# PSUM banks dealt in turn in an attention stage: maxima and short work share four banks, values' products in halves, the first maxima four heads at once

## The chip, the cores and the metric

The kernel runs on one core of a Trainium2 chip as a single launch. The metric is the device time of that launch in microseconds, the median over several runs; lower is better. One execution was also recorded by the hardware profiler. In the text PE is TensorE, PEld its weight loads, DVE VectorE, ACT ScalarE, POOL GpSimd and SP SyncE.

## The reference

A network of eight sublayers works on x (4 batches of 512 tokens, 512 features). Each sublayer is added as x + tanh(g) · sublayer(layernorm(x)). The seventh, called stage 6 in the kernel, is the one that changes. It is attention of each batch's 512 tokens to 512 context tokens, with 32 heads of 16 features and a rotary position on queries and keys:

```python
q = (x @ Wq).reshape(b, n, 32, 16)
k, v = jnp.split(ctx @ Wkv, 2, axis=-1)        # each (b, 512, 32, 16)
q = apply_axial_rope(q, pos_map)
k = apply_axial_rope(k, ctx_pos_map)
logits = jnp.einsum('bqhd,bkhd->bhqk', q, k) * 0.25
w = jax.nn.softmax(logits, axis=-1)
attn = jnp.einsum('bhqk,bkhd->bqhd', w, v).reshape(b, n, 512)
return attn @ Wout + bout

x = x + jnp.tanh(g_xattn[3]) * _L3_xattn_ref(_layernorm(x), ctx, pos, pos, Wq, Wkv, Wout, bout)
```

## The kernel before

Stages 0 to 5 come first, stage 7 (a mixture of experts) after it. Everything is float32. Keys and values of stage 6 are worked out in earlier stages and lie in DRAM as k6 and v6. The results of stage 5 lie in DRAM too: its last block is scattered there by an indirect DMA from GpSimd's queue (s_ys from s_yb), and stage 6 loads them per 128 tokens (s_y from s_ys, a buffer of two tiles) and adds them to x (L729).

**Start.** `pieces(b)` yields the short work that makes a batch's queries: `results` (load and add stage 5's results, then `lnstats`, whose inverse square root is a Newton iteration on DVE), `xT` (normalise on DVE at L1576, transpose into ptx), `query` (product pq, then rope on DVE, L1427 to L1429) and `queryT` (transpose into ptq, copied on ACT into qT). For batch 0 all pieces run ahead of the loop; for batch b+1 they are handed out between the slots of batch b.

**Softmax.** Logits are needed twice. `maxima` computes them with the queries on the partitions (s_ps, 128x512 per head and 128 queries), and DVE takes each row's maximum, negated, into `top` (L1656). When a group of four heads is through, `turn` transposes these maxima (ptm) and adds them to the queries' transpose qT (L1631) in a spare feature. The second time the logits come with the keys on the partitions and the maximum already taken off (s_pl), and ACT takes their exps into pr (L1766). `weigh` multiplies the exps by the values (s_av, an accumulation over the four key tiles, with a column of ones for the sums), ACT copies av to oT, and `norm` transposes it (pt), takes the reciprocal of the sums (L1703) and multiplies (L1704). `project` (ptr) and `projected` (po) apply the output matrix; bias and residual follow on DVE (L1724, L729).

**Loop.** Per batch there are eight groups g of four heads, in each four key tiles k, in each two slots (i = 1, then 0): 64 slots. A slot issues together two logits products for two heads and two maxima products of a group twelve slots ahead (LEAD = 12). Each of the four has a contraction of 32 rows and sits in its own quarter of PE's rows. The program order on PE is fixed for everything that goes through `together` (products and values' products); transpositions and projections are placed by the scheduler. Ahead of the loop the twelve first pairs of maxima run alone.

`later` holds the values' product of a key tile, flushed in the next slot with i = 1. `behind` holds norm, project and projected, flushed two at a time in slots with i = 0.

**Banks.** Of PSUM's eight banks of 128x512 float32 the maxima have three (tag sc, with ptx, ptq and the queries of batch 0), the logits three (pl), all other short work one (mm: ptm, pt, ptr, po, pq of later batches), av one. Two waits are written out by hand: a slot's first product waits for the first exp and the first maximum of the slot before:

```python
self.together(parts + more, list(freed) + exps[-2:-1])   # freed is freed[-2:-1]
```

Transposed maxima, normalised averages and the rest have a bank of their own, so a bank in which DVE still reads one of them holds up no maximum.

Of the kernel before, what the change touches and what calls it, by code (L numbers as in the profile page):

```python
# [9 lines left out]
F32 = mybir.dt.float32  # L10
# [38 lines left out]
class Net:  # L49
# [116 lines left out]
    def lnstats(self, name, tiles, key="", root=True):  # L166


        nc = self.nc
        n = len(tiles)  # L170
        mv = self.s(f"mv_{name}", 2 * n, f"mv{n}{key}")
        mv = mv.rearrange("p (t k) -> p t k", k=2)
        for i, x in enumerate(tiles):
            st = self.s(f"st_{name}_{i}", 6, "st")
            nc.vector.bn_stats(st, x)
            nc.vector.bn_aggr(mv[:, i, :], st)
        rs = self.s(f"rs_{name}", n, f"rs{n}{key}")
        if root:
            nc.scalar.activation(rs, mv[:, :, 1], AF.Sqrt, bias=self.eps[1e-5])
            nc.vector.reciprocal(rs, rs)  # L180
            return mv, rs
        v, y = self.s(f"nv_{name}", n, "nv"), self.s(f"ny_{name}", n, "ny")
        nc.vector.tensor_scalar(v, mv[:, :, 1], 1e-5, None, op0=ALU.add)
        ints = rs.bitcast(I32)
        nc.vector.tensor_scalar(ints, v.bitcast(I32), 1, None, op0=ALU.logical_shift_right)
        nc.vector.tensor_scalar(ints, ints, -1, 0x5F3759DF, op0=ALU.mult, op1=ALU.add)
        for _ in range(4):
            nc.vector.tensor_tensor(y, rs, rs, op=ALU.mult)
            nc.vector.tensor_tensor(y, y, v, op=ALU.mult)
# [33 lines left out]

    def transposed(self, name, src, dst, i=0, tied=False):

        pt = self.mm(f"ptr_{name}")
        for c in range(4):
            ins = self.nc.tensor.transpose(
                pt[:, c * P : (c + 1) * P], src[:, c * P : (c + 1) * P], self.ident
            ).ins  # L230
            if tied:
                self.tie(ins)
        self.evict(i, dst, pt.rearrange("p (c n) -> p c n", c=4))
# [1300 lines left out]
    def s6(self):  # L1534
# [13 lines left out]

        bank = lambda name: self.ps3.tile([P, S], F32, tag="sc", name=f"s6_{name}")

# [7 lines left out]
        def pieces(b):  # L1558
# [3 lines left out]
            made[b] = kT, qT, va  # L1562
            for y in range(2):
                nc.sync.dma_start(kT[y], self.k6[b][:, 4 * y : 4 * y + 4, :])
            nc.sync.dma_start(va, self.v6[b].rearrange("(k p) n -> p k n", p=P))
            xs = self.x[b * TB : (b + 1) * TB]
# [20 lines left out]
            def query(t):  # L1587
                if b:
                    pq = self.mm(f"s6_pq_{b}_{t}")
                else:  # L1590

                    pq = bank(f"pq_{b}_{t}")
                self.chain(pq, [(room["xT"][:, c, cols(t)], wq[:, c, :]) for c in range(DC)])
                self.rope(f"q_{b}_{t}", pq, b * TB + t, ropes[t % 2])

            def results():

                self.combine("s5", self.wt5, range(b * TB, (b + 1) * TB))
                stats[b] = self.lnstats(
                    f"s6_{b}", self.x[b * TB : (b + 1) * TB], f"s6{b}", root=False  # L1600
                )
# [16 lines left out]
        def maxima():  # L1618

            freed = []  # L1620

            def turn(b, g):
                qT = made[b][1][g // 4]
                pt = self.mm(f"s6_ptm_{b}_{g}")
                for t in range(TB):
                    nc.tensor.transpose(
                        pt[:, t * P : (t + 1) * P],
                        top[g % 2][:, t].rearrange("p j k -> p (j k)"),
                        self.ident,
                    )  # L1630
                nc.vector.tensor_tensor(qT[:, g % 4, :], qT[:, g % 4, :], pt, op=ALU.add)  # L1631

            waiting = None
            for b in range(NB):
                kT, qT = made[b][0:2]
                for g in range(8):
                    for t in range(TB):
                        for y in range(2):
                            if waiting and t == 1:
                                turn(*waiting)  # L1640
                                waiting = None
                            ps = [bank(f"ps_{b}_{g}_{t}_{y}_{i}") for i in range(2)]
                            parts = []
                            for i in range(2):
                                rows = slice(32 * (2 * y + i), 32 * (2 * y + i + 1))
                                parts.append((
                                    ps[i],
                                    qT[g // 4][rows, g % 4, t * P : (t + 1) * P],
                                    kT[g // 4][rows, g % 4, :],
                                    dict(start=True, stop=True),  # L1650
                                ))

                            def after(ps=ps, dst=top[g % 2][:, t, 2 * y : 2 * y + 2, 16:17]):
                                for i in range(2):
                                    with self.tc.high_priority():
                                        ins = nc.vector.tensor_reduce(  # L1656
                                            dst[:, i], ps[i], axis=AX.X, op=ALU.max, negate=True
                                        ).ins
                                    freed.append(ins)

                            yield parts, freed[-2:-1], after
                    waiting = b, g
            turn(*waiting)

        behind, later = Behind(), Behind()
        avs, o4s, exps = {}, {}, []

        def flush(what, n=None):
            last, what.waiting = what.waiting[:n], what.waiting[n:] if n else []
            for f, args in last:  # L1670
                f(*args)

        def weigh(b, g, k, prs):

            va = made[b][2]
            if k == 0:
                avs[g] = self.ps1.tile([P, S], F32, tag="av", name=f"s6_av_{b}_{g}", bufs=1)
            parts = []
            for j in range(4):
                h = 4 * g + j  # L1680
                parts.append((
                    avs[g][32 * j : 32 * (j + 1), :],
                    va[:, k, 17 * h : 17 * h + 32],
                    prs[j // 2][:, j % 2, :],
                    dict(start=(k == 0), stop=(k == TB - 1)),
                ))
            self.together(parts)
            if k == TB - 1:
                oT = self.t(f"s6_oT_{b}_{g}")
# [3 lines left out]
        def norm(b, g, oT):  # L1693
            if g == 0:
                o4s[b] = self.up.tile([P, TB, D], F32, tag="o", name=f"s6_o_{b}")
            po = self.mm(f"s6_pt_{b}_{g}")
            for t in range(TB):
# [15 lines left out]
        def project(b, t):  # L1713
            oT = self.t(f"s6_oTT_{b}_{t}").rearrange("p (c n) -> p c n", c=DC)
            self.transposed(f"s6_o_{b}_{t}", o4s[b][:, t, :], oT, 1)
            behind(projected, b, t, oT, more=True)
# [3 lines left out]
        def projected(b, t, oT):  # L1720
            po = self.mm(f"s6_po_{b}_{t}")
            self.chain(po, [(oT[:, c, :], wo[:, c, :]) for c in range(DC)])
# [4 lines left out]
        for piece in pieces(0):  # L1727
            piece()
        nc.sync.dma_start(wo, a["s6_wo"].rearrange("(c p) n -> p c n", p=P))
        beside = maxima()  # L1730
        for _ in range(LEAD):
            parts, freed, after = next(beside)
            self.together(parts, freed)
            after()
        for b in range(NB):
# [4 lines left out]
            for g in range(8):  # L1740
                y, gi = g // 4, g % 4
                for k in range(TB):
                    prs = [None, None]
                    for i in (1, 0):


                        pl = [
                            self.ps3.tile([P, S], F32, tag="pl", name=f"s6_pl_{b}_{g}_{k}_{i}_{j}")
                            for j in range(2)
                        ]  # L1750
                        parts = []
                        for j in (2 * i, 2 * i + 1):
                            rows = slice(32 * j, 32 * (j + 1))
                            parts.append((
                                pl[j % 2],
                                kT[y][rows, gi, k * P : (k + 1) * P],
# [3 lines left out]
                        more, freed, after = next(beside, None) or ([], [], None)  # L1760
                        self.together(parts + more, list(freed) + exps[-2:-1])
                        prs[i] = self.up.tile(
                            [P, 2, S], F32, tag="pr", name=f"pr_s6_{b}_{g}_{k}_{i}", bufs=4
                        )
                        for j in range(2):
                            exps.append(nc.scalar.activation(prs[i][:, j, :], pl[j], AF.Exp).ins)  # L1766
# [85 lines left out]
def kernel(ctx: ExitStack, tc: tile.TileContext, a: dict, out: bass.AP):  # L1852
# [122 lines left out]
```

## Time and profile before

| | us |
|---|---|
| median of 3 runs | 3399.83 (3399.31 to 3401.43) |
| profiled execution | 3401.39 |
| its span in the profile | 3399.4 |
| stage 6: from the last scatter of stage 5 to the last projection | 2254 to 3014 |
| batches 0 to 3 of the loop begin at | 2342.1, 2501.1, 2670.9, 2840.7 |
| mean granted TensorE clock | 0.92 |

Busy in the whole span: PE 2880.1 (85%), PEld 1432.3 (42%), DVE 1975.8 (58%), ACT 1197.1 (35%), POOL 627.9 (18%). The profiled execution is 1.6 us above the median of the runs; sums are made against its own time. In a group of instructions the line gives busy time, mean ns of one, and the idle time of the engine just before with the instruction that ended it. In a timeline a line is: start, duration, engine, line of the kernel, output from inputs, shape, count, and in brackets the idle time before and what ended it.

### The profile page before, as it was taken

What the parts mean: (1) busy time and instruction counts of PE and PEld (TensorE: products, weight loads), DVE (VectorE), ACT (ScalarE), POOL (GpSimd) and SP (SyncE); (2) the same over time, 40 slices, a digit from 0 to 9 for tenths busy, and PEclk for the clock granted to TensorE, in tenths of its full rate; (3) what the DMA queues carried; (4) which work ended last, traced back from release to release, by engine and by line L of the source; (5) the groups of instructions that cost most, each with busy time, mean ns of one, the idle gap of its engine ahead of it and who ended that gap; (6) DMA issues with size and microseconds to landing.
All of it is one profiled execution on the core that took longest, in us unless ns stands there. A gap on an engine that the chain in (4) does not pass through costs nothing.

```text
span 3399.4 us, 39917 instructions
## 1 busy us (share of the span) xinstructions
PE 2880.1 (85%) x14620; PEld 1432.3 (42%) x14624; DVE 1975.8 (58%) x3148; ACT 1197.1 (35%) x1927; POOL 627.9 (18%) x509
## 2 busy tenths in 40 slices
PE   4889898968998989998836699968898988889995
PEld 2333333223444444444414588842233332244673
DVE  5555555558797989975687311137666666634103
ACT  1243333355544454433222111112544444520231
POOL 0000000005564655760000122210000000000341
PEclk9799999988998999999967699987999999989997
DMA  3000000047675876861212599971000000022698
GB/s 125 7 1 7 1 1 9 1 160 227 195 230 177 241 223 202 250 188 57 84 63 85 177 324 325 325 250 50 13 27 13 27 1 1 1 75 78 245 385 314
DMA packets 266338, 438.56 MB, mean 129 GB/s; under 512 B 32368, under 2 KB 114544, under 8 KB 264608
## 3 DMA queue, kind: packets, MB, share of 16 engines
q1 hardware_dynamic: 247776, 382.52, 35.3%
q0 software_dynamic: 13760, 45.10, 3.7%
q10 hardware_dynamic: 4608, 8.39, 0.7%
q8 instruction: 117, 1.92, 0.2%
q14 instruction: 77, 0.63, 0.1%
HBM read 370.79 MB, written 65.13 MB: 128 GB/s over the span
## 4 chain that ended last, share of the span: by engine, by line
PE 38%; DVE 9%; issue 3%; DMA 2%; POOL 2%; ACT 1%; SPq 0%; POOLq 0%; DVEq 0%; ACTq 0%
PE s_po L238 8%; PE s_pl L262 7%; PE pg_s L238 6%; PE s_av L262 4%; DVE s_top L1656 2%; PE s_ph L238 2%; PE s_pq L238 2%; PE s_ps L262 1%; PE s_pkv L238 1%; PE s_pr L238 1%; DVE x L729 1%; DMA s_y<-s_ys 1%; PE pt_s L218 1%; POOL s_ys L1321 1%; PE s_pb L238 1%
## 5 line engine op out<-in xcount | busy, mean ns | idle before, releaser
L1012 POOL TENSOR_TENSOR s_h<-s_h,s_C 128x512 f32<-128x512 f32 x256 | 447.2, 1747 | 295.7 <-DVE s_h L1011 249.7
L1656 DVE TENSOR_REDUCE s_top<-s_ps 128x1 f32<-128x512 f32 x512 | 330.1, 686 | 162.6 <-PE s_ps L262 158.4
L1766 ACT ACTIVATE pr_s<-s_pl 128x512 f32<-128x512 f32 x512 | 277.9, 595 | 344.2 <-PE s_ps L262 327.1
L1011 DVE TENSOR_TENSOR_SCAN s_h<-s_da,s_db 128x512 f32<-128x512 f32 x256 | 312.0, 1219 | 62.8 <-PE s_y L262 37.1
L262 PE MATMUL s_pl<-s_qT,s_kT 32*128 32x512 f32 x1024 | 291.4, 642 | 63.4 <-DVE s_top L1656 59.0
L262 PE MATMUL s_ps<-s_kT,s_qT 32*128 32x512 f32 x1024 | 306.6, 668 | 6.1 <-DVE s_top L1656 5.8
L1010 ACT ACTIVATE s_da<-s_rdl,s_A 128x512 f32<-128x512 f32 x256 | 184.3, 722 | 329.3 <-DVE s_h L1011 328.7
L238 PE MATMUL s_ph<-xT_s,s_wu 128*128 128x256 f32 x1024 | 250.4, 400 | 0.7 <-ACT xT_s L161 0.7
L771 PE MATMUL s_acc<-s_wd,s_hT 128*128 128x512 f32 x512 | 239.9, 612 | 6.8 <-ACT s_hT L802 6.8
L238 PEld LDWEIGHTS s_ph<-xT_s,s_wu 128*128 128x128 f32 x1024 | 199.9, 200 | 79.3 <-issue 48.4
L238 PEld LDWEIGHTS pg_s<-s_xbT,s_w 128*128 128x128 f32 (+1 forms) x1872 | 214.1, 183 | 19.8 <-issue 17.8
L599 DVE TENSOR_REDUCE s_nmx<-ps_s 128x2 f32<-128x992 f32 x128 | 151.4, 1184 | 116.7 <-PE ps_s L262 116.7
L238 PE MATMUL pg_s<-s_xbT,s_w 128*128 128x128 f32 (+1 forms) x1872 | 215.7, 275 | 1.4 <-ACT s_xbT L161 1.4
L262 PE MATMUL s_av<-pr_s,s_v 128*32 128x512 f32 (+1 forms) x1536 | 209.6, 617 | 0.8 <-ACT pr_s L1766 0.7
L1009 DVE TENSOR_TENSOR s_db<-s_B,s_rdu 128x512 f32<-128x512 f32 x256 | 202.7, 792 | 10.5 <-DMA s_B<-s_bc 2.7
L714 ACT ACTIVATE pr_s<-pl_s 128x1024 f32<-128x1024 f32 (+1 forms) x128 | 130.9, 1022 | 192.1 <-PE pl_s L262 161.7
L262 PE MATMUL s_y<-s_h,ident 64*64 64x512 f32 x1024 | 146.5, 635 | 47.1 <-issue 30.0
L1400 DVE TENSOR_TENSOR g_s<-g_s,pg_s 128x256 f32<-128x256 f32 x78 | 27.5, 353 | 263.9 <-ACT g_s L1399 263.9
L262 PEld LDWEIGHTS s_pl<-s_qT,s_kT 32*128 32x128 f32 x1024 | 80.0, 184 | 232.9 <-ACT pr_s L1766 197.7
L262 PE MATMUL pl_s<-s_qT,s_kT 32*128 32x512 f32 (+1 forms) x512 | 151.1, 667 | 26.1 <-ACT pr_s L714 23.0
L262 PE MATMUL ps_s<-s_kT,s_qT 32*128 32x496 f32 x512 | 156.1, 713 | 4.5 <-DVE s_nmx L599 4.1
L771 PEld LDWEIGHTS s_acc<-s_wd,s_hT 128*128 128x128 f32 x512 | 93.4, 192 | 151.9 <-issue 116.4
(376 smaller groups left out, 4269.7 us busy)
## 6 DMA issues: line engine op xcount, KB each, us to landing
s_B<-s_bc SPq DMA_DIRECT2D x256, 256.0 KB
s_C<-s_bc SPq DMA_DIRECT2D x256, 256.0 KB
s_w<-in_s_wg SPq DMA_DIRECT2D x39, 704.0 KB
s_w<-in_s_wu SPq DMA_DIRECT2D x39, 704.0 KB
s_w_rt<-in_s_ru SPq DMA_DIRECT2D x47, 512.0 KB
s_w_rt<-in_s_rd SPq DMA_DIRECT2D x47, 512.0 KB
s_w<-in_s_wd SPq DMA_DIRECT2D x39, 512.0 KB
s_y<-s_ys SPq DMA_DIRECT2D x32, 512.0 KB
```

The lines of the kernel that those rows point to most:

```text
L218: nc.tensor.transpose(pt[:, i * P : (i + 1) * P], xl[i][:, c * P : (c + 1) * P], self.ident)
L238: ins = self.nc.tensor.matmul(out, lhsT=l, rhs=r, start=(i == 0), stop=(i == len(pairs) - 1)).ins
L262: ins = self.nc.tensor.matmul(out, lhsT=l, rhs=r, **flags).ins
L599: i = nc.vector.tensor_reduce(nmx[:, at : at + 2], ps[:, :, 0:M], axis=AX.X, op=ALU.max, negate=True,)
L714: nc.scalar.activation(prs[i][0:n], pl[0:n], AF.Exp)
L771: ins = nc.tensor.matmul(accs[i][t], lhsT=hT[:, j, t * P : (t + 1) * P], rhs=wd[f // 4][:, f % 4, :], start=(f == 0), stop=(f == FC - 1),).ins
L1009: nc.vector.tensor_tensor(db, br, du, op=ALU.mult)
L1010: nc.scalar.activation(da, dl, AF.Exp, scale=am[:, e, n : n + 1])
L1011: nc.vector.tensor_tensor_scan(h, da, db, 0.0, op0=ALU.mult, op1=ALU.add)
L1012: nc.gpsimd.tensor_tensor(h, h, cr, op=ALU.mult)
L1656: ins = nc.vector.tensor_reduce(dst[:, i], ps[i], axis=AX.X, op=ALU.max, negate=True).ins
L1766: exps.append(nc.scalar.activation(prs[i][:, j, :], pl[j], AF.Exp).ins)
```

## The change

Seven edits, all in stage 6 except the first, which is in a helper that stage 6 uses:

- the Newton iteration of `lnstats` has three steps instead of four;
- the loads of keys and values of a batch are issued behind the loads of stage 5's results, not ahead of them;
- the tag sc has four banks and is dealt in turn to the maxima and to all short work (ptx, pq, ptq, ptm, pt, ptr, po); the tag mm is gone from the stage;
- the waits written out by hand name the reader of the very bank that a product takes (`dealt` and `read` keep the books), where that reader is a maximum or an exp;
- the twelve first pairs of maxima run as six double pairs, four heads at once, with the second pair of heads in the banks of the logits;
- the values' product of a key tile is issued as two halves of 256 tokens, one in each of the two slots that follow;
- in every slot one entry of `later` and one of `behind` is flushed.

```diff
-        for _ in range(4):
+        for _ in range(3):
...
-    def transposed(self, name, src, dst, i=0, tied=False):
+    def transposed(self, name, src, dst, i=0, tied=False, room=None):
-        pt = self.mm(f"ptr_{name}")
+        pt = (room or self.mm)(f"ptr_{name}")
...
-        bank = lambda name: self.ps3.tile([P, S], F32, tag="sc", name=f"s6_{name}")
+        banks = {"sc": 4, "pl": 3}
+        readers = {tag: [] for tag in banks}
+        def dealt(name, tag="sc"):
+            at = len(readers[tag])
+            readers[tag].append(None)
+            old = readers[tag][at - banks[tag]] if at >= banks[tag] else None
+            t = self.ps3.tile([P, S], F32, tag=tag, name=f"s6_{name}", bufs=banks[tag])
+            return t, (tag, at), [old] if old is not None else []
+        def read(where, ins):
+            readers[where[0]][where[1]] = ins
+        bank = lambda name: dealt(name)[0]
...
-            for y in range(2):
-                nc.sync.dma_start(kT[y], self.k6[b][:, 4 * y : 4 * y + 4, :])
-            nc.sync.dma_start(va, self.v6[b].rearrange("(k p) n -> p k n", p=P))
...
-                if b:
-                    pq = self.mm(f"s6_pq_{b}_{t}")
-                else:
-                    pq = bank(f"pq_{b}_{t}")
+                pq = bank(f"pq_{b}_{t}")
...
             def results():
                 self.combine("s5", self.wt5, range(b * TB, (b + 1) * TB))
+                for y in range(2):
+                    nc.sync.dma_start(kT[y], self.k6[b][:, 4 * y : 4 * y + 4, :])
+                nc.sync.dma_start(va, self.v6[b].rearrange("(k p) n -> p k n", p=P))
...
-                pt = self.mm(f"s6_ptm_{b}_{g}")
+                pt = bank(f"ptm_{b}_{g}")
...
-                            ps = [bank(f"ps_{b}_{g}_{t}_{y}_{i}") for i in range(2)]
+                            ps = [
+                                dealt(f"ps_{b}_{g}_{t}_{y}_{i}", "pl" if alone[0] and y else "sc")
+                                for i in range(2)
+                            ]
...
-                                    freed.append(ins)
-                            yield parts, freed[-2:-1], after
+                                    read(ps[i][1], ins)
+                            yield parts, olds, after
...
-        def weigh(b, g, k, prs):
+        def weigh(b, g, k, prs, half):
+            cols = slice(half * (S // 2), (half + 1) * (S // 2))
...
-            po = self.mm(f"s6_pt_{b}_{g}")
+            po = bank(f"pt_{b}_{g}")
...
-            self.transposed(f"s6_o_{b}_{t}", o4s[b][:, t, :], oT, 1)
+            self.transposed(f"s6_o_{b}_{t}", o4s[b][:, t, :], oT, 1, room=bank)
...
-            po = self.mm(f"s6_po_{b}_{t}")
+            po = bank(f"po_{b}_{t}")
...
-        for _ in range(LEAD):
-            parts, freed, after = next(beside)
-            self.together(parts, freed)
-            after()
+        for _ in range(LEAD // 2):
+            two = [next(beside) for _ in range(2)][::-1]
+            self.together(
+                [p for parts, _, _ in two for p in parts], [i for _, old, _ in two for i in old]
+            )
+            for _, _, after in two:
+                after()
...
-                        self.together(parts + more, list(freed) + exps[-2:-1])
+                        self.together(parts + more, freed + pl[0][2] + pl[1][2])
...
-                        if i == 1:
-                            flush(later)
-                            later(weigh, b, g, k, prs, more=True)
-                        else:
-                            idle = not behind.waiting
-                            flush(behind, 2)
-                            if idle and todo:
-                                todo.pop(0)()
+                        flush(later)
+                        if i == 0:
+                            for half in range(2):
+                                later(weigh, b, g, k, prs, half, more=True)
+                        idle = not behind.waiting
+                        flush(behind)
+                        if idle and i == 0 and todo:
+                            todo.pop(0)()
...
-    with net.pools(wp=2, kq=4, vp=2, up=1, rp=1, tp=8, bp=1, sp=2, ps3=3, ps1=1):
+    with net.pools(wp=2, kq=4, vp=2, up=1, rp=1, tp=8, bp=1, sp=2, ps3=4, ps1=1):
```

More of the change, by code (lines that the diff above doesn't have):

```diff
@@ L1618, in maxima @@
         def maxima():
-            freed = []
             def turn(b, g):
                 qT = made[b][1][g // 4]
-                pt = self.mm(f"s6_ptm_{b}_{g}")
+                pt = bank(f"ptm_{b}_{g}")
                 for t in range(TB):
@@ L1641, in maxima @@
                                 waiting = None
-                            ps = [bank(f"ps_{b}_{g}_{t}_{y}_{i}") for i in range(2)]
-                            parts = []
+                            ps = [
+                                dealt(f"ps_{b}_{g}_{t}_{y}_{i}", "pl" if alone[0] and y else "sc")
+                                for i in range(2)
+                            ]
+                            parts, olds = [], []
                             for i in range(2):
+                                olds += ps[i][2]
                                 rows = slice(32 * (2 * y + i), 32 * (2 * y + i + 1))
                                 parts.append((
-                                    ps[i],
+                                    ps[i][0],
                                     qT[g // 4][rows, g % 4, t * P : (t + 1) * P],
@@ L1656, in after @@
                                         ins = nc.vector.tensor_reduce(
-                                            dst[:, i], ps[i], axis=AX.X, op=ALU.max, negate=True
+                                            dst[:, i], ps[i][0], axis=AX.X, op=ALU.max, negate=True
                                         ).ins
-                                    freed.append(ins)
-                            yield parts, freed[-2:-1], after
+                                    read(ps[i][1], ins)
+                            yield parts, olds, after
                     waiting = b, g
@@ L1665, in s6, with flush @@
         behind, later = Behind(), Behind()
-        avs, o4s, exps = {}, {}, []
-        def flush(what, n=None):
-            last, what.waiting = what.waiting[:n], what.waiting[n:] if n else []
+        avs, o4s = {}, {}
+        def flush(what):
+            last, what.waiting = what.waiting[:1], what.waiting[1:]
             for f, args in last:
                 f(*args)
-        def weigh(b, g, k, prs):
+        def weigh(b, g, k, prs, half):
             va = made[b][2]
-            if k == 0:
+            cols = slice(half * (S // 2), (half + 1) * (S // 2))
+            if k == 0 and half == 0:
                 avs[g] = self.ps1.tile([P, S], F32, tag="av", name=f"s6_av_{b}_{g}", bufs=1)
@@ L1681, in weigh @@
                 parts.append((
-                    avs[g][32 * j : 32 * (j + 1), :],
+                    avs[g][32 * j : 32 * (j + 1), cols],
                     va[:, k, 17 * h : 17 * h + 32],
-                    prs[j // 2][:, j % 2, :],
-                    dict(start=(k == 0), stop=(k == TB - 1)),
+                    prs[j // 2][:, j % 2, cols],
+                    dict(start=(k == half == 0), stop=(k == TB - 1 and half == 1)),
                 ))
             self.together(parts)
-            if k == TB - 1:
+            if k == TB - 1 and half == 1:
                 oT = self.t(f"s6_oT_{b}_{g}")
@@ L1729, in s6 @@
         nc.sync.dma_start(wo, a["s6_wo"].rearrange("(c p) n -> p c n", p=P))
+        alone = [True]
         beside = maxima()
-        for _ in range(LEAD):
-            parts, freed, after = next(beside)
-            self.together(parts, freed)
-            after()
+        for _ in range(LEAD // 2):
[5 more added lines that the diff above has]
+                after()
+        alone[0] = False
         for b in range(NB):
@@ L1744, in s6 @@
                     for i in (1, 0):
[L1747 to L1750, printed above, removed]
+                        pl = [dealt(f"pl_{b}_{g}_{k}_{i}_{j}", "pl") for j in range(2)]
                         parts = []
@@ L1754, in s6 @@
                             parts.append((
-                                pl[j % 2],
+                                pl[j % 2][0],
                                 kT[y][rows, gi, k * P : (k + 1) * P],
@@ L1765, in s6 @@
                         for j in range(2):
-                            exps.append(nc.scalar.activation(prs[i][:, j, :], pl[j], AF.Exp).ins)
+                            ins = nc.scalar.activation(prs[i][:, j, :], pl[j][0], AF.Exp).ins
+                            read(pl[j][1], ins)
                         if after:
                             after()
-                        if i == 1:
-                            flush(later)
-                            later(weigh, b, g, k, prs, more=True)
-                        else:
-                            idle = not behind.waiting
-                            flush(behind, 2)
-                            if idle and todo:
-                                todo.pop(0)()
+                        flush(later)
[6 more added lines that the diff above has]
+                            todo.pop(0)()
                         slot += 1
```

## Prediction

> **What bounds the kernel now.** I read the page first, then the busy time by stretch, then the chain of waits around stage 6, then the timeline of single slots. TensorE is busy 85% of the span, but stage 6 (2254 to 3014 us) is not bound by its arithmetic.
>
> First, the busy time by stretch: start of the stage, first maxima, batches 0 to 3 of the main loop, tail. The columns are stretch and length, busy us of PE, weight loads, VectorE, ScalarE and GpSimd, then granted clock, DMA share and GB/s.
>
> ```profile
> 2254.00:2283.00 29.00, 0.00 (x0) 0.00 (x0) 13.07 (x37) 0.00 (x0) 2.89 (x5) 0.56 0.85 309
> 2308.00:2342.00 34.00, 27.17 (x55) 7.08 (x53) 24.45 (x57) 2.12 (x3) 0.00 (x0) 0.51 0.24 77
> 2342.00:2501.00 159.00, 135.84 (x899) 43.74 (x899) 109.52 (x225) 79.34 (x147) 0.00 (x0) 0.97 0.02 7
> 2501.00:2671.00 170.00, 152.65 (x964) 51.99 (x965) 108.21 (x189) 82.54 (x153) 0.00 (x0) 1.00 0.06 20
> 2841.00:2988.00 147.00, 129.46 (x836) 39.24 (x830) 81.82 (x136) 76.53 (x141) 0.00 (x0) 1.00 0.00 1
> ```
>
> The reader sees that no engine fills a batch: VectorE has 108 of 170 us, ScalarE 82. The order of the work and the turn of the banks set the pace.
>
> Second, two plain slots and the values' product between them, from the timeline of batch 0, and one slot of the last batch that has no maxima:
>
> ```profile
> 2440.97 0.70 PE L262 MATMUL s_pl<-s_qT,s_kT 32*128 32x512 f32 x2
> 2442.12 1.08 ACT L1766 ACTIVATE pr_s<-s_pl 128x512 f32<-128x512 f32 x2 [1.01 <-PE s_ps L262]
> 2442.21 1.29 DVE L1656 TENSOR_REDUCE s_top<-s_ps 128x1 f32<-128x512 f32 x2 [0.81 <-PE s_ps L262]
> 2443.05 0.70 PE L262 MATMUL s_pl<-s_qT,s_kT 32*128 32x512 f32 x2 [0.94 <-DVE s_top L1656]
> 2444.12 1.06 PE L262 MATMUL s_av<-pr_s,s_v 128*32 128x512 f32 x8
> 2445.11 0.70 PE L262 MATMUL s_pl<-s_qT,s_kT 32*128 32x512 f32 x2
> ...
> 2966.48 1.13 PE L262 MATMUL s_pl<-s_qT,s_kT 32*128 32x512 f32 x4 [0.68 <-ACT pr_s L1766]
> ```
>
> A slot's four products ("quad") occupy PE for 2444.12 − 2443.05 = 1.07. A slot without a values' product waits for the first maximum of the slot before and takes 2443.05 − 2440.97 = 2.08; one with it takes 1.07 + 0.99 = 2.06. So a plain group of 8 slots takes 16.59 (2440.97 to 2457.56). Where only the exps bind, the next quad follows after 2966.48 − 2964.68 = 1.80 (the earlier quad stands at 2964.68 in the same timeline).
>
> Third, what a quad costs when something comes between its halves (batch 1):
>
> ```profile
> 2516.19 1.13 PE L262 MATMUL s_pl<-s_qT,s_kT 32*128 32x512 f32 x4
> 2517.25 0.66 PE L228 MATMUL ptr_s_o<-ident,s_o 128*128 128x128 f32 x4
> 2518.29 0.44 PE L1584 MATMUL s_ptx<-ident,s_xl 128*128 128x128 f32 x2 [0.38 <-DVE s_xl L1576]
> 2518.66 1.12 PE L262 MATMUL s_ps<-s_kT,s_qT 32*128 32x512 f32 x2
> ```
>
> Logits and maxima no longer share the array: each pair takes its own 1.06 to 1.12.
>
> Fourth, the chain of waits through the start and the first maxima, and the same kind of scatter in stage 7:
>
> ```profile
> 2254.67 6.67 DMA s_ys<-s_yb,s_to
> 2261.97 6.15 DMA s_y<-s_ys
> 2271.88 4.37 DMA s_y<-s_ys
> 2313.46 2.13 PE s_ps L262 x4
> 2315.59 0.68 DVE s_top L1656
> 2316.32 2.13 PE s_ps L262 x4
> ```
>
> The twelve first slots go one after another, 2316.32 − 2313.46 = 2.86 each, at a clock of 0.51.
>
> **The change part by part.**
>
> *Start.* The k and v loads of batch 0 (1 MB and more) now stand behind the four result loads on SP's queue. The last scatter took 6.67 beside them; in stage 7 such a scatter alone took 2.73 (chain, 3358.99). The loads from 2261.97 on share the queues too (stretch: 309 GB/s). One Newton step fewer is four VectorE operations of 0.20 on the chain: 0.8. I take −5: the scatter's 3.9 and the 0.8, rounded for what the result loads gain. Bounds −1 (only the Newton step; the scatter was slow for its own reasons) and −9 (the later loads gain as well). What is moved back: kT at 2308 and va at the first values' product, some 30 us of cover; without it their own landing, about 5. Later batches' loads move behind their results with most of a batch (170 us) of cover: nothing, or the same 5 without it. SP's queue there holds only these, and POOL's has nothing but scatters that are over.
>
> *First maxima.* 34.0 now (2308.09 to 2342.1). Six double slots replace twelve; four row groups run at once. The Trainium skill ("TensorEngine Tiling (Array Packing)", Theoretical Speedup) promises up to four times with 32-row tiles, where two run now: that would halve the stretch to 17.0. The row says otherwise: 24 maxima at the loop's pitch of 0.61 are 14.7, and VectorE has some 8 of other work in the stretch (24.45 busy less 24 × 0.686 of the page's row; residuals, normalisation of batch 1), so VectorE becomes the bound at 22.7. I take −11.3 and not −17; bounds −8 and −15. The queries before it lose about 0.5 (banks in turn).
>
> *Main loop: plain groups.* I worked the order of PE's, VectorE's and ScalarE's instructions in both programs through with the trace's durations (a product starts when PE is free, its inputs are made and its bank was read). For before this gives 161.0, 169.0, 169.0 for batches 0 to 2 and 170.4 for batch 3 to the last product; the trace has 159.0, 169.8, 169.8 and 173.25.
>
> In the changed program a group deals 18 tiles in turn to four banks: a a b b pt c c d d e e f f ptm g g h h (two maxima a slot, pt the transposed averages, ptm the transposed maxima). Banks alone would help: slots a, e, d, h find theirs free, and halves of the values' product (0.5 each; bounds 0.50 to 0.65, the page's 128x256 and 128x512 products at 400 and 612 ns) fit in the slack 1.80 − 1.07. A group would take about 15.0.
>
> But the order puts pt inside the quad of slot c: logits, one transpose, maxima, three transposes. The first half waits for the copy of the averages on ScalarE, behind two exps; once it is there, slot c costs 1.06 + 0.2 + 1.05 + 0.43 + half a product 0.5 = 3.24. And slot d's second maximum takes pt's bank: it waits for the reciprocal and the product of the averages (L1703, L1704), which VectorE has behind slot c's two maxima. Those begin 2.47 after c: 2.47 + 1.22 + 0.28 + 0.57 = 4.54 after c, 1.30 into d; d costs 1.30 + 1.05 + 0.5 = 2.85. Behind the waiting maximum on PE stand d's half product and slot e; the exps wait for e.
>
> The sum: a 1.80, b 2.08, c 3.24, d 2.85, e 1.80, f 2.08, g 1.80, h 1.80 = 17.45, against 16.59. By the same rule before gives 16.4, so the difference is 0.9 to 1.03 a group. There are 27 such splits with maxima in them (before: 2 split quads in all).
>
> *Main loop: all.* By the rule after takes 172.5, 178.3, 178.3, and 175.9 to the last product: +11.5, +9.3, +9.3, +5.5 = +35.6. By kind: 14 groups with nothing else +14.4; the groups that also carry the next batch's queries or the last one's projection +24.0, since their tiles (read for up to 2.3 us by rope or residual) now stand in the turn of the maxima and no longer in a bank of their own; the tail −2.8, since with four banks the next transposition need not wait for the residual's addition.
>
> *Halves and the array's mode.* The quad runs 32-row tiles, the values' product 128-row ones; halves double the switches, 256 more. The skill (same page, Key Properties) says that a change of mode drains TensorE, which speaks against this change. The row: the product starts 1.07 after its quad and the next quad 0.99 after it, so no more than some 0.05 is visible. By the rule, 256 × 0.05 = +13; by the row's slack (1.80 − 1.57 = 0.23 in unsplit slots) nothing. I take nothing and keep +13 for the range.
>
> *Sum.* +35.6 − 11.3 − 5.0 − 0.5 = +18.8 on the profiled execution (3401.39, span 3399.4): 3420.2. That execution is 1.6 above the median of 3399.83; the median becomes 3418.6, say **3419**. The terms' bounds (start ±4, maxima ±4, plain groups 27 × 0.13 = 3.5, the rule's own misfit of some 3 a batch) make 3407 to 3433 for this case.
>
> **Rivals.**
>
> 1. *The split costs little (faster).* If the reciprocal of the averages gets through before slot c's maxima, slot d does not wait: 27 × 1.05 = 28 less, 3391. If the split vanished wholly, 27 × 2.45 = 66 less, 3353. For it: ScalarE and VectorE have slack, and only two split quads show in the trace. Against it: 2516.19 shows both pairs at full length, and VectorE's order has the reciprocal behind. It decides from 0.7 saved per pair of slots c and d (19 / 27). Chance 0.18.
>
> 2. *A wash.* Start and first maxima at their far bounds give −24, and the loop's shared banks cost 10 less than worked out: within 7 of 3400. Chance 0.12.
>
> 3. *Worse.* Halves cost 0.65 and drain: up to +20, 3439. Chance 0.10.
>
> 4. *It does not do what it says.* The banks are in turn, but the first maxima could still run by twos: the second pair takes the logits' banks, and the order keeps the four adjacent, so I give it only +11, inside the range.
>
> **How the numbers follow.** The forecast has 0.60. A measurement of this kernel can tell about 0.2%, 6.8 us. Faster by more: rival 1, 0.18. Within: rival 2, 0.12. Slower: the forecast and rival 3, 0.70. The range runs from rival 1's 3391 (only the wait gone) to rival 3's 3439; about 0.08 is left below and 0.08 above.
>
> **What would show it.** Start: the last scatter near 3, first query near 5 us earlier. First maxima: 22 to 23 us, VectorE without gaps. Plain group of batch 0: 17.4, with transposes between a slot's logits and its maxima, and in the next slot a maximum that waits for L1704. Batches 172, 178, 178. Tail shorter by 3. Wrong it is if plain groups take 15 to 16.4 us, or if the maxima of slot d start at once.

## The result and the profile after

The changed kernel takes 3386.64 us (median of 6 runs, 3383.0 to 3392.07); the kernel before took 3399.3 beside it (6 runs). The ratio is 0.9962, with a 95% interval of 0.9951 to 0.9973: faster by 0.38%, where the prediction had 3419 and a range from 3391. The profiled execution has a span of 3385.4.

First the chain of waits through the start of stage 6, the counterpart of the one shown of before:

```profile
2249.14 2.71 DMA s_ys<-s_yb,s_to
2251.86 3.73 DMA s_y<-s_ys
2259.34 4.89 DMA s_y<-s_ys
2270.47 3.67 PE s_ptx L1595 x16
```

The last scatter is down from 6.67 to 2.71 and the first result load from 6.15 to 3.73. From the scatter's start to the first transposition it is 21.33 us, against 28.61 before (2254.67 to 2283.28). On SP's queue the first key load stands behind two of the four result loads only, not behind all of them; it is issued at 2252.79, when the scatter has landed.

Then the busy time by stretch: start, queries, first maxima, batches 0, 1 and 2 of the loop.

```profile
2249.14:2270.47 21.33, 0.00 (x0) 0.03 (x1) 12.30 (x33) 0.00 (x0) 2.88 (x5) 0.57 0.81 297
2270.47:2291.37 20.90, 20.90 (x73) 11.97 (x73) 18.19 (x46) 4.67 (x9) 0.00 (x0) 0.87 0.74 272
2291.37:2314.13 22.76, 15.41 (x62) 5.13 (x61) 21.05 (x47) 3.19 (x5) 0.00 (x0) 0.61 0.30 92
2314.13:2478.54 164.41, 151.47 (x1148) 51.82 (x1148) 114.56 (x232) 78.92 (x147) 0.00 (x0) 0.95 0.05 14
2478.54:2653.25 174.71, 168.79 (x1217) 59.99 (x1217) 107.42 (x189) 81.97 (x153) 0.00 (x0) 0.99 0.06 20
2653.25:2831.05 177.80, 171.89 (x1217) 61.37 (x1217) 107.41 (x189) 81.97 (x153) 0.00 (x0) 0.97 0.04 13
```

VectorE now fills the first maxima (21.05 of 22.76), and PE fills the batches: 168.79 of 174.71, where before it had 152.65 of 170. So the bound of the loop moved from the turn of the banks to PE itself, and PE is busy for longer, since products that shared the array now run apart. The stage by parts, both profiles (for the loop, from the first logits to the start of the last projection's first product):

| us | before | after | difference | predicted |
|---|---|---|---|---|
| start: scatter to first transposition | 28.6 | 21.3 | −7.3 | −5.0 |
| queries of batch 0 | 24.8 | 20.9 | −3.9 | −0.5 |
| first maxima | 34.0 | 22.8 | −11.2 | −11.3 |
| loop | 668.2 | 684.6 | +16.4 | +35.6 |
| stage 6 | 755.6 | 749.6 | −6.0 | +18.8 |

The line between queries and first maxima lies elsewhere in the two programs: before, the last queries are transposed ahead of the first maxima; after, they are transposed among them (from 2294.61 on). So the two rows are safest read as one: 58.8 before, 43.7 after, −15.1 for −11.8.

By batch the loop differs by +5.3, +4.9, +8.0 and −1.8. Part of this is the clock and not the order of the work. The first groups of batches 1 and 2, after:

```profile
2478.54:2512.47 33.93, 33.01 (x180) 12.20 (x180) 16.93 (x29) 12.32 (x23) 0.00 (x0) 1.00 0.20 65
2653.25:2690.23 36.98, 36.05 (x181) 13.52 (x181) 16.93 (x29) 12.32 (x23) 0.00 (x0) 0.91 0.19 60
```

PE does the same work in the same order, but the granted clock is 0.91 instead of 1.00: it falls to 0.50 for some 7 us (2678.7 to 2685.5), and the group takes 3.0 longer. Two shorter dips lie in the fourth groups of batches 1 and 2 (20.5 each at 0.92). In `strict` and `forced` below that group takes 2.34 more than a plain one, which would make 19.1 here, so I estimate 1.4 for each dip. Before, there is one, in the tail: its first projection takes 5.40 where the three others take 3.70. So some 4 of the 16.4 are dips (5.8 less 1.7). They are not peculiar to the new loop; the profile of `b_first` below, which has the loop of before, has one as well (31.5 in the first group of batch 2, at 0.84, against 26.7). What brings them on is not shown.

The difference of the two profiles is 14.0, that of the medians 12.7. In this pair of profiles −5.5 of it lies ahead of stage 6 and −2.5 behind the start of the last projection (386.6 to the end of the span, against 389.2). Over the twelve profiles of this study the last scatter of stage 5 began between 2248.1 and 2257.3, and the part from the last projection on took 382 to 391, so neither can be put down to the change. The stage explains 6 of the 12.7 (interval 9.2 to 16.6), or 10 without the dips; the rest is not assigned to a part of the change.

Now the place where the prediction expected the wait. Timeline of slots c and d of a plain group in batch 0 (one transposition of pt inside the quad, at 2433.18):

```profile
2432.12 1.13 PE L262 MATMUL s_pl<-s_qT,s_kT 32*128 32x512 f32 x4 [0.37 <-DVE s_top L1670]
2433.18 0.33 PE L1716 MATMUL s_pt<-ident,s_oT 128*128 128x128 f32 x1
2433.44 1.13 PE L262 MATMUL s_ps<-s_kT,s_qT 32*128 32x512 f32 x4
2434.50 0.55 PE L1716 MATMUL s_pt<-ident,s_oT 128*128 128x128 f32 x3
2434.98 0.64 PE L262 MATMUL s_av<-pr_s,s_v 128*32 128x256 f32 x8
2435.55 0.70 PE L262 MATMUL s_pl<-s_qT,s_kT 32*128 32x512 f32 x2
2435.56 0.70 PE L262 MATMUL s_ps<-s_kT,s_qT 32*128 32x512 f32 x2
2435.81 0.25 DVE L1720 RECIPROCAL s_ri<-s_pt 128x16 f32<-128x16 f32 x1
2436.09 0.42 DVE L1721 TENSOR_TENSOR s_o<-s_pt,s_ri 128x256 f32<-128x256 f32 x1
2437.36 0.70 PE L262 MATMUL s_pl<-s_qT,s_kT 32*128 32x512 f32 x2
```

Slot c is split as predicted and takes 2435.55 − 2432.12 = 3.43 (predicted 3.24). Slot d takes 1.81 (predicted 2.85): both of its maxima start at 2435.56, before VectorE has even begun to read pt. They don't stand on pt's bank. The built program shows why. In this group pt has bank 0, slot c's maxima have banks 1 and 2, slot d's have 3 and 1, slot e's 2 and 0: slot d's second maximum gets the bank of slot c's first maximum, and pt's bank goes to a maximum of slot e. The banks of one tag are not handed out in the order of the calls, as I had taken from the word "dealt". So the books of `dealt` and `read`, which count in the order of the calls, do not always name the reader of the very bank that a product takes, though the list of edits says so.

A plain group is then 16.77 (16.59 before), all of it in terms of the prediction: 17.45 + 0.19 (c) − 1.04 (d) + 0.15 (f, 2.23) = 16.75.

### The profile page after: what moved, and what is told of

Same layout as the page of the kernel before. It is cut to its first block, busy times and chain, and to the rows that moved or that the text cites. A ratio compares the mean times of both kernels' runs of the same rounds, so it can differ in the third digit from the quotient of the medians.

```text
span 3385.4 us, 41976 instructions
## 1 busy us (share of the span) xinstructions
PE 2917.4 (86%) x15644; PEld 1452.6 (43%) x15648; DVE 1972.4 (58%) x3132; ACT 1196.0 (35%) x1927; POOL 626.0 (18%) x509
## 4 chain that ended last, share of the span: by engine, by line
PE 37%; DVE 7%; issue 4%; ACT 2%; POOL 2%; DMA 2%; SPq 0%; POOLq 0%; ACTq 0%; DVEq 0%
PE s_po L238 8%; PE s_pl L262 8%; PE pg_s L238 6%; PE s_av L262 2%; PE s_pq L238 2%; PE s_ps L262 2%; ACT pr_s L1786 2%; PE s_ph L238 2%; POOL s_ys L1321 1%; DMA s_y<-s_ys 1%; DVE x L729 1%; DVE s_top L1670 1%; POOL s_xb L1294 1%; PE s_pr L238 1%; PE s_pkv L238 1%
## 5 line engine op out<-in xcount | busy, mean ns | idle before, releaser
L262 PE MATMUL s_av<-pr_s,s_v 128*32 128x256 f32 (+2 forms) x2560 | 238.7, 445 | 0.2
L1294 POOL DMA_INDIRECT s_xb<-s_xs,s_from x86 | 83.2, 967 | 378.4 <-PE ptr_s_xb L228 232.4
```

What stands on the lines that cost most here:

```text
L262: ins = self.nc.tensor.matmul(out, lhsT=l, rhs=r, **flags).ins
L1294: self.nc.gpsimd.indirect_dma_start(out=t, out_offset=None, in_=self.sorted[name][1], in_offset=bass.IndirectOffsetOnAxis(ap=fr[:, j : j + ...
```

## The experiments

### The predicted program itself

`strict` makes the turn real:

```diff
-            t = self.ps3.tile([P, S], F32, tag=tag, name=f"s6_{name}", bufs=banks[tag])
+            own, n = (f"sc{at % 4}", 1) if tag == "sc" else (tag, banks[tag])
+            t = self.ps3.tile([P, S], F32, tag=own, name=f"s6_{name}", bufs=n)
```

> The changed kernel with the four banks as four tags of one buffer each, so that they really go in turn; with that the scheduler puts the transposed averages (pt) behind the quad of slot c and no longer inside it. Theory (the prediction's wait in slot d never came because the pool handed out another bank; where the bank is shared the wait is real): the maximum of slot d waits for L1721, d is about 2.8 instead of 1.81, c falls from 3.43 to 2.1, a plain group is about 16.4 against 16.77, the run about 3377. Rival (the wait is hidden anyway, VectorE gets through in time): d stays at 1.81, a group is 15.4, the run 3350.

Measured: 3372.32, ratio 0.9917 (0.9904 to 0.9930), a plain group 16.40. Slot d in its timeline:

```profile
2434.80 0.70 PE L262 MATMUL s_pl<-s_qT,s_kT 32*128 32x512 f32 x2
2434.81 0.69 PE L262 MATMUL s_ps<-s_kT,s_qT 32*128 32x512 f32 x1
2435.27 0.42 DVE L1722 TENSOR_TENSOR s_o<-s_pt,s_ri 128x256 f32<-128x256 f32 x1
2435.84 1.09 PE L262 MATMUL s_ps<-s_kT,s_qT 32*128 32x512 f32 x2
2437.43 0.70 PE L262 MATMUL s_pl<-s_qT,s_kT 32*128 32x512 f32 x2
```

One maximum starts with the logits (2434.81, x1), the other only at 2435.84 (x2), after L1722 has read pt: d takes 2.63. So the wait is real where the bank is shared. But the quad of slot c is whole here, and c falls to 2.23; the run comes out a little below the expected 3377. To get wait and split at once, `forced` puts the transpositions there by hand:

```diff
...
+                        now, pend[:] = list(pend), []
+                        if now:
+                            self.together(parts, freed + pl[0][2] + pl[1][2])
+                            turned(*now[0][0:2], [0])
+                            self.together(more)
+                            turned(*now[0][0:2], [1, 2, 3])
...
```

> The program that the prediction reckoned with: the banks really in turn (as in 'strict') and the transposed averages put inside the quad of slot c by hand, behind the logits, so that slot d's second maximum stands on their bank. Theory (the one wrong step was that the changed kernel has this wait): c 3.4, d 2.9 to 3.0, a plain group 17.7 to 18.0 against 16.77, 28 groups about +31, the run 3411 to 3420, as predicted for the changed kernel. Rival (the wait of slot d is hidden even there, or later slots catch up): a group 16.4 to 16.9, the run 3372 to 3390.

Measured: 3412.45, ratio 1.0038 (1.0027 to 1.0048), a plain group 17.66. The same two slots:

```profile
2439.48 1.13 PE L262 MATMUL s_pl<-s_qT,s_kT 32*128 32x512 f32 x4 [0.37 <-DVE s_top L1671]
2440.79 1.13 PE L262 MATMUL s_ps<-s_kT,s_qT 32*128 32x512 f32 x4
2442.91 0.69 PE L262 MATMUL s_ps<-s_kT,s_qT 32*128 32x512 f32 x1
2443.44 0.42 DVE L1726 TENSOR_TENSOR s_o<-s_pt,s_ri 128x256 f32<-128x256 f32 x1
2444.01 1.09 PE L262 MATMUL s_ps<-s_kT,s_qT 32*128 32x512 f32 x2
2445.60 0.70 PE L262 MATMUL s_pl<-s_qT,s_kT 32*128 32x512 f32 x2
```

c is 3.42 and d 2.70, a little less than the 2.9 expected, since only the second maximum is late and the rest of the quad has run. Its loop takes 708.3, 40.1 more than before; the prediction had 35.6 for the changed kernel. So the sum came near for a program in which the banks go in turn and pt splits the quad, and the changed kernel is not that program. It is not exact: `forced` has 30 such splits where the changed kernel has 27.

`forced` and `strict` both have the banks in turn and differ in where pt stands, inside the quad or behind it. That is 17.66 − 16.40 = 1.26 a group, and 40 us of the runs: what the split costs by itself.

### What the split costs

`unsplit` moves the transpositions behind the quad:

```diff
-                nc.tensor.transpose(po[:, ts], oT[:, ts], self.ident)
+                self.tie(nc.tensor.transpose(po[:, ts], oT[:, ts], self.ident).ins)
...
+                        idle = not behind.waiting
+                        flush(behind)
                         flush(later)
...
-                        idle = not behind.waiting
-                        flush(behind)
```

> The changed kernel with one entry of behind flushed ahead of later and the transposed averages tied into PE's order, so that they stand behind the quad and in a bank that is next used two slots on. Theory (the split quad is what the changed loop still pays: c is 3.43, of which 1.3 is the maxima's products run apart from the logits): c falls to 2.1, a plain group from 16.77 to 15.2 to 15.5, 28 groups give -36 to -43, the run 3344 to 3351. Rival (the pace is set by the exps and maxima, the split only moves idle time): a group stays above 16.4, the run above 3375.

Measured: 3340.08, ratio 0.9825 (0.9813 to 0.9838), a plain group 15.30. Its slot c:

```profile
2428.74 0.70 PE L262 MATMUL s_pl<-s_qT,s_kT 32*128 32x512 f32 x2
2428.75 0.70 PE L262 MATMUL s_ps<-s_kT,s_qT 32*128 32x512 f32 x2
2429.81 0.66 PE L1716 MATMUL s_pt<-ident,s_oT 128*128 128x128 f32 x4
2430.40 0.64 PE L262 MATMUL s_av<-pr_s,s_v 128*32 128x256 f32 x8
2430.97 0.70 PE L262 MATMUL s_pl<-s_qT,s_kT 32*128 32x512 f32 x2
```

c is 2.23 instead of 3.43, which is 1.20 of the 1.47 that a plain group gains (16.77 − 15.30). The other 0.27 is slot b (1.81 for 2.08), and it does not come from the split. With this edit the averages ask for their bank one slot later, behind slot c's maxima; in the built program slot c then takes the two banks of slot a, and no longer one whose maximum belongs to slot b. The run gains 46.6 us on the changed kernel. In the profiles the loop gains 51.1 (684.6 to 633.5): 25 of it are the 17 plain groups, the rest lies in the groups with other work, some 6 of it the dips of the clock, which the loop of this profile does not have. The rival (pace of the exps) falls: 1.81 a slot is their pace, and the split came on top of it.

> 'unsplit' with the banks really in turn, so that the waits written by hand name the true reader. Theory (with the averages behind the quad their bank is next used two slots on, so its order no longer matters): plain group 15.3 as in 'unsplit', the run 3335 to 3345. Rival (waits on the reader of another bank cost something in 'unsplit'): a group at most 15.0, the run at most 3332.

`unsplit` with the edit of `strict`: 3336.05, ratio 0.9809 (0.9790 to 0.9828), a plain group 15.29 to 15.30. As the theory has it, the order of the banks does not matter once nobody stands behind pt: the intervals of both overlap.

> 'unsplit' with three buffers instead of two for stage 5's results and one scratch tile fewer (seven). Theory (in the first group of batch 0 the maxima stand 4.0 behind a residual that waits for a result load, which waits for a buffer): that wait goes, the first group falls from 32.1 to about 28, the run about 3336. Rival (the scratch tile is missed, or the load comes no earlier): 3340 or more.

`unsplit` with `net.y2 = 3` and `tp=7`: 3338.33, ratio 0.9816 (0.9794 to 0.9838). The first group of batch 0 stays at 32.2 (32.1 in `unsplit`), against the theory. The wait for the load, 5.24 in the chain of waits of `unsplit`, is gone; in its place the chain has residuals, statistics and maxima on VectorE one after another, so VectorE's own work is the bound there. `strict`, `unsplit` and its two variants all beat both kernels.

### Halves, and a bank of its own for the short work

`a_whole` issues a key tile's product in one piece:

```diff
...
-                            for half in range(2):
-                                later(weigh, b, g, k, prs, half, more=True)
+                            later(weigh, b, g, k, prs, 1, more=True)
...
-            cols = slice(half * (S // 2), (half + 1) * (S // 2))
+            cols = slice(0, S)
...
```

> The changed kernel with the values' product of a key tile in one piece of 512 tokens, in one slot of two. Theory (a half fits in the 0.73 that the exps leave after a quad, a whole of 0.99 does not): the slots with it take 2.06 instead of 1.80, a plain group about 17.2 against 16.77, the run about 3399. Rival (halves cost more than they save, 0.57 each and twice the changes of shape on PE): a group at most 16.7, the run at most 3386.

Measured: 3399.31, ratio 1.0004 (0.9993 to 1.0015), a plain group 17.18. Halves bring 0.41 a group with the quads split, some 12 us a run, although two halves take 1.14 (0.57 each, 2430.40 to 2430.97 above) and a whole 0.99. The comparison is not quite of halves alone: in `a_whole` pt splits the quad of slot b (2.86) and not of slot c.

`a_own` gives ptm, pt, ptr, po and later pq the tag mm again, and the maxima three banks.

```diff
-        banks = {"sc": 4, "pl": 3}
+        banks = {"sc": 3, "pl": 3}
...
-            po = bank(f"pt_{b}_{g}")
+            po = self.mm(f"s6_pt_{b}_{g}")
...
```

> The changed kernel with three banks for the maxima and a bank of its own for ptm, pt, ptr, po and later pq, as before; halves, start and double first maxima as changed; no split quads except two. Theory (the fourth bank is what takes the pace of a slot from 2.08 to 1.80; without it the halves bring nothing): 8 slots of 2.08, a plain group 16.6, the first maxima slow as in 'b_both', the run 3381 to 3388. Rival (halves and unsplit quads do it, the fourth bank is not needed): a group near 15.3, the run below 3360.

Measured: 3397.6, ratio 0.9992 (0.9985 to 0.9999), a plain group 16.82: the theory of the fourth bank holds (nothing near 15.3; from the first transposition to the first logits 53.3, as in `b_both` below), but the run is 10 us above my number. Two things I had left out. The halves leave no slot free for short work: a slot with pt or ptm takes 1.07 + 0.57 + 0.57 = 2.21 instead of 2.08 (0.13 twice a group). And in batch 1 the four groups with queries and projection take 107.4, as many as in the changed kernel (107.7), where before they took 102.7. `unsplit`, with shared banks, has 99.5 there. So it is not the shared banks, as the prediction had it, that make these groups dear; what does is not shown.

### Start and first maxima, one by one on the kernel before

`b_first` moves only the key and value loads behind `combine`; `b_lead` takes only the double first maxima:

```diff
...
-        for _ in range(LEAD):
-            parts, freed, after = next(beside)
-            self.together(parts, freed)
-            after()
+        for _ in range(LEAD // 2):
+            two = [next(beside) for _ in range(2)][::-1]
+            self.together([p for parts, _, _ in two for p in parts], two[0][1])
+            for _, _, after in two:
+                after()
...
```

`b_both` has both, and three Newton steps.

> The kernel before with only the result loads ahead of keys and values (four Newton steps, first maxima by twos). Theory: scatter 2.7, 21 to 22 us from its start to the first transposition instead of 28.6, all of it kept, the run 3390 to 3393. Rival (chance): no change, 3396 to 3401.

> The kernel before with only the double first maxima (second pair of heads in the logits' banks); keys and values loaded ahead of the results as before. Theory (the slow last scatter of 6.67 comes from the key load beside it): the scatter is again above 6, from its start to the first transposition 28 us; the first maxima win the 5.5 of 'b_both' (three banks), 2 go in the first group, the run 3394 to 3397. Rival (the slow scatter of the one profile was chance): scatter near 2.7, 21 us to the first transposition, the run as 'b_both' (3385).

> The kernel before with only the start and the first maxima changed: results loaded ahead of keys and values, three Newton steps, six double pairs in the banks of maxima and logits. Theory: start -7 and first maxima -15 as in the trace of the changed kernel, 3 to 5 given back in the first group, the run about 3381, faster than the changed kernel (3386.6), whose loop loses some 16 against them. Rival (the loop's banks bring part of the gain, the start's gain is chance of one profile): the run 3388 or more.

Measured: `b_first` 3391.28, ratio 0.9983 (0.9975 to 0.9991); `b_lead` 3389.85, ratio 0.9980 (0.9971 to 0.9989); `b_both` 3384.64, ratio 0.9951 (0.9937 to 0.9964). The scatter of `b_lead`, with the old order of loads, and of `b_first`, from their chains of waits:

```profile
2251.07 6.88 DMA s_ys<-s_yb,s_to
```

```profile
2248.09 2.71 DMA s_ys<-s_yb,s_to
```

6.67 and 6.88 with the key load beside it, 2.71 or 2.72 in all ten profiles with the loads moved: the scatter's slowness comes from the order of the loads, not from chance. From its start to the first transposition `b_first` takes 22.9, a little more than expected, and `b_lead` 28.9.

The first maxima need the fourth bank to win their 11 us. Double slots of `b_both` (three banks) and then of the changed kernel:

```profile
2313.60 2.09 PE L262 MATMUL s_ps<-s_kT,s_qT 32*128 32x512 f32 x8 [1.57 <-DVE s_top L1660]
2317.78 2.09 PE L262 MATMUL s_ps<-s_kT,s_qT 32*128 32x512 f32 x8 [1.69 <-DVE s_top L1660]
```

```profile
2300.04 2.09 PE L262 MATMUL s_ps<-s_kT,s_qT 32*128 32x512 f32 x8 [0.56 <-DVE s_top L1670]
2303.17 2.09 PE L262 MATMUL s_ps<-s_kT,s_qT 32*128 32x512 f32 x8 [1.03 <-DVE s_top L1670]
```

One every 4.18 against one every 3.13. `a_own`, the changed kernel with three banks, takes 36.1 for its first maxima, as `b_both` does, against 22.8. From the first transposition to the first logits it is 58.8 before, 53.3 in `b_both`, 52.5 in `b_lead`, 43.7 in the changed kernel. `b_lead` was expected at 3394 or more and came out lower: it gained 6.3 instead of 5.5 there and gave back 0.6 in the first group instead of 2.

`b_both` lies between its theory (about 3381) and the rival (3388 or more), and is as fast as the changed kernel, within 2 us: the gain of the changed kernel is that of the start and the first maxima. What four banks win in the queries and first maxima (53.3 − 43.7 = 9.6), the changed loop loses again and more (684.6 − 668.4 = 16.2 in these profiles, some 6 of it dips of the clock).

## Why the prediction was wrong

- *Start, first maxima.* Right in mechanism. VectorE bounds the first maxima (busy 21.05 of 22.76), and not the factor that the prediction quoted for row tiling, as it said. That 22.76 meets 22.7 so closely is luck: the stretch after has the last queries' rope and transpositions in it, which lay in the stretch ahead of it before. For both stretches together the sum was low (−15.1 for −11.8). The start was sized low too (−7.3 for −5): the result loads behind the scatter gained, 6.15 to 3.73, which I had rounded to nothing.
- *Plain groups, slot c.* Right: the split, its place and nearly its size (3.43 for 3.24), in 27 slots.
- *Plain groups, slot d: the step that failed.* "Slot d's second maximum takes pt's bank". It does not; the pool hands out another, and slot d takes 1.81 and not 2.85. The wait was priced at 2.85 − 1.81 = 1.04 a group, 28 us over 27 groups. Against it c and f (the slot with ptm) were sized low by 0.19 and 0.15, 5 and 4 us. −28 + 9 = −19, and the loop came out at +16.4 for +35.6. That this fits to the microsecond is luck, since some 4 of the 16.4 are dips of the clock: without them the loop came out at about +12. `strict` and `forced` show the mechanism: where pt's bank is shared, d takes 2.63 and 2.70, and `forced`, with the split and the wait, takes 3412, inside the prediction's range for its forecast.
- *Loop, all.* The +24.0 of the groups with queries and projection came out near in sum (about +20) only because some 6 of that are dips of the clock, and it was put down to the wrong cause. With shared banks and whole quads these groups take 99.5 − 4 × 15.3 = 38.3 a batch beyond plain ones (`unsplit`), before 102.7 − 4 × 16.6 = 36.3, so sharing costs about 2 a batch in this comparison. Five quads are split by other short work (three by po, two by ptx and ptm). The last batch gained 1.8 where +5.5 was predicted. 1.7 of that is the dip in the tail before; the waits of its six splits, which did not come, are 6 × 1.04 = 6.2 and are about the rest.
- *Halves and the array's mode.* A half was taken at 0.5 and takes 0.57 (2434.98 to 2435.55); two are 0.15 more than a whole. In a slot with slack nothing of it shows: it keeps the exps' 1.81. In slots c and f, which have none, it is part of what was sized low. Whether the drain that the prediction weighed is in these 0.07 is not shown; the next product still starts 1.07 after its quad begins, and `a_whole`, with fewer changes, is slower.
- *Rivals.* Rival 1 in its first form (only slot d's wait gone, 3391) is what happened, 4 us further, but for another reason: VectorE's reciprocal does stand behind slot c's maxima (2435.81), and nobody waits for it. Its second form (the split costs nothing) is refuted by `unsplit`, and by `forced` against `strict`.

## What to carry to other kernels

A wait on a buffer is a wait on the buffer that the tile is given, not on the one that the calls suggest: read the bank of each tile in the built program before pricing a wait over dozens of slots. Where four small products share the array, a full-width instruction that the scheduler puts between them can be costly: here 1.2 to 1.3 us each time. Tying it behind the quad, which also moved its bank by a slot, won 46 us, more than the whole change. A split of work to fill the slack of slots takes the slack from whatever short work lived there.

## What was not expected of the hardware

A scatter of 128 rows took 6.67 and 6.88 us with a 1 MB load beside it and 2.71 or 2.72 without, in twelve profiles with no exception. And the start of the last scatter varied by 9 us between the ten kernels that have no key load ahead of it and are the same up to there (2248.1 to 2257.3), more than most of the effects studied. The granted clock fell to 0.50 for 3 to 10 us in the midst of the loop (2677.5 to 2687.7 in `b_first`), in some profiles and not in others.
